# A Mamba scan beside a mixture of experts: some C products on GpSimd, and the carried state through the scan's initial value

## The chip, the cores and the metric

One core of a Trainium2 chip runs the whole program. The metric is the device time of one execution in microseconds. The runs shown took 687.11, 687.22 and 687.6 us, with a median of 687.22. One more execution was profiled; it took 687.01 us.

## The reference, cut to what matters

The input has 4 sequences of 512 steps with 256 features. The kernel computes `x + layernorm(mamba(layernorm(x)))` and then, on that, `x + layernorm(moe(layernorm(x)))`. The part that the change touches is the state-space scan of the Mamba layer (512 channels, 16 states each):

```python
def step(state, inp):
    dt_t, x_t, B_t, C_t = inp
    dA = jnp.exp(dt_t[..., None] * A)
    dBx = dt_t[..., None] * B_t[:, None, :] * x_t[..., None]
    state = state * dA + dBx
    y = jnp.einsum('bds,bs->bd', state, C_t)
    return (state, y)
```

The experts (16 with a router that keeps 4, and a shared one) compute `silu(x @ w1) * (x @ w3)`, weighted by the router and multiplied by `w2`. Every layer norm needs a mean and `(variance + eps) ** -0.5` of each row.

## The kernel before

**Blocks and slots.** The 2,048 steps are cut into 8 blocks of 256 steps (`n`); two blocks make one sequence, so the odd blocks 1, 3, 5 and 7 start from the state that the block before them left, and the even ones from zero. A block's 512 x 16 states are worked off in 32 slots (`k`). One slot is a tile of 128 partitions (32 channels times 4 states) with two columns (`j` = 0 and 1) of 256 steps, laid one behind the other.

**One slot.** `exps` (line 535, ScalarE) writes the decay `exp(dt * A)` into a PSUM tile `h`, one instruction per column, and clears the first element of column 1 (line 538), so that one scan over 512 elements restarts at the second column. `inputs_of` (line 547, GpSimd) makes `dbx`, the product of dt times x with B, for two slots at a time. `scan` (line 830, VectorE) runs in place over `h` with a start value of 0.0. `times_c` (line 838, VectorE) multiplies by C into an SBUF tile `hc`, and `sum_y` (line 852, TensorE) adds up the states. `close` and `gated_y` (lines 864 and 870) finish a group of 128 channels.

**The carried state.** In even blocks `keep` (line 842, ScalarE) copies the last element of each column into `carry`. In odd blocks `decay0`, `decay1` and `delta` (lines 817 to 824, GpSimd, ScalarE, GpSimd) multiply that state by the first decay, once for each group of 8 slots, and line 549 (GpSimd) adds the result to the first element of each `dbx` column.

**Rings.** Only three `h` tiles exist (`RINGS`, line 49), so `exps` of slot k + 3 waits for the last reader of slot k's tile, the product with C. `hc` has 11 buffers, `dbx` 3. The expert matmuls' PSUM tiles `h1` and `h3` have one buffer each.

**Around the scan.** `front(n)` prepares a block (norm, input projection, convolution, softplus). `chain(n)` follows a block's last slot: output projection, a norm, the residual, a second norm, a transposition, the router. Then `experts(n)` runs ten pairs of experts: `hidden` (line 1094, TensorE) twice, Tanh and copy (lines 1101 to 1106, ScalarE), a weight product and a gate product (lines 1109 and 1116, GpSimd) with one on VectorE between them (line 1113), and `down` (line 1129, TensorE). Experts of block n run beside the slots of block n + 1. The norms' statistics come from VectorE (line 383), and `rstd_of` makes scale and offset with four small GpSimd operations (lines 389 to 392), at 30 places.

**The order.** Every piece of work is a task with an engine, an expected duration, a rank and the tasks it depends on. The list `ORDER` (lines 58 to 215) writes out the sequence of all tasks; each engine, and the SyncE queue of DMAs, works off its part of this sequence strictly in order. `Plan.order` also models start times, from which only one thing follows: in front of the first `down`, spare matmuls (`warm`, line 355) are put where the model sees TensorE idle.

Of the kernel before, what the change touches and what calls it, by code (L numbers as in the profile page):

```python
# [14 lines left out]
P = 128  # L15
# [35 lines left out]
    tail=4, bt=2, ct=2, xg=2, rep=3, delta=3, h=3, dbx=3, hc=11, yg=2, o=1, xn2=1, xn_t2=2, lg=2,  # L51
# [7 lines left out]
    28, 304, 310, 307, 306, 305, 309, 29, 32, 314, 30, 308, 24, 311, 319, 33, 315, 15, 25, 313, 40,  # L59
    34, 320, 14, 26, 312, 31, 317, 35, 108, 324, 316, 1591, 70, 37, 12, 329, 36, 321, 27, 328, 41,  # L60
    1592, 322, 323, 325, 333, 71, 38, 330, 42, 327, 342, 72, 318, 326, 147, 39, 331, 73, 341, 334,
    43, 351, 74, 109, 332, 346, 343, 44, 303, 335, 110, 1568, 344, 1599, 336, 350, 45, 361, 381,
    347, 111, 47, 352, 345, 355, 75, 370, 340, 76, 348, 48, 16, 356, 349, 360, 337, 49, 78, 353,
    354, 358, 77, 112, 357, 79, 365, 362, 113, 369, 363, 51, 366, 80, 364, 52, 338, 384, 423, 374,
    54, 367, 371, 368, 359, 383, 375, 393, 55, 372, 376, 385, 378, 117, 339, 148, 373, 388, 57, 85,
    56, 386, 379, 377, 389, 392, 403, 58, 62, 60, 387, 86, 390, 46, 394, 53, 59, 382, 63, 50, 87,
    391, 396, 397, 380, 64, 61, 81, 412, 395, 466, 402, 398, 404, 82, 114, 149, 115, 1600, 399, 400,
    407, 65, 83, 426, 465, 405, 100, 411, 408, 1607, 116, 84, 413, 406, 410, 416, 120, 424, 409,
    101, 417, 425, 401, 414, 419, 121, 102, 468, 435, 418, 89, 415, 430, 122, 420, 427, 103, 434,
    445, 503, 139, 431, 429, 150, 421, 428, 118, 140, 454, 436, 90, 439, 91, 186, 432, 88, 433, 438,  # L70
    469, 141, 444, 470, 440, 119, 437, 124, 472, 446, 449, 441, 442, 1569, 450, 125, 142, 1608, 447,
    479, 448, 453, 443, 126, 451, 66, 458, 455, 452, 156, 471, 153, 459, 151, 152, 456, 487, 457,
    461, 67, 128, 460, 475, 68, 462, 473, 69, 478, 104, 127, 505, 422, 463, 476, 464, 467, 614, 474,
    1570, 105, 494, 480, 129, 482, 540, 477, 154, 506, 1571, 486, 507, 481, 1572, 483, 130, 490,
    106, 1573, 509, 484, 107, 155, 488, 92, 1693, 493, 1618, 491, 504, 485, 93, 1574, 489, 157, 495,
    516, 492, 496, 497, 1575, 95, 143, 187, 542, 158, 1576, 577, 498, 508, 182, 94, 499, 1577, 510,
    188, 512, 98, 1578, 500, 511, 1579, 513, 97, 144, 1580, 515, 145, 1581, 524, 99, 1582, 514,
    1583, 225, 519, 517, 1593, 189, 501, 520, 531, 1595, 1594, 1584, 523, 518, 1601, 1617, 1596,
    543, 527, 96, 544, 1585, 521, 146, 1597, 1586, 1603, 1602, 525, 579, 1587, 183, 546, 528, 530,
    1588, 1598, 526, 1589, 580, 184, 1590, 534, 1627, 522, 1604, 553, 529, 615, 131, 535, 545, 1609,  # L80
    532, 132, 1605, 1613, 533, 502, 1606, 547, 581, 561, 536, 549, 548, 178, 550, 552, 136, 1611,
    179, 551, 133, 138, 1610, 180, 1628, 537, 554, 556, 568, 190, 1612, 560, 1619, 1623, 555, 185,
    557, 191, 1637, 1614, 564, 163, 562, 195, 1620, 1615, 565, 1629, 583, 164, 558, 1633, 134, 538,
    563, 1638, 567, 1616, 165, 137, 135, 566, 590, 571, 541, 569, 159, 582, 572, 1643, 657, 1630,
    539, 559, 570, 192, 598, 584, 160, 1639, 573, 586, 161, 574, 585, 1624, 589, 587, 167, 578,
    1634, 1621, 588, 591, 605, 168, 193, 592, 1647, 593, 597, 1622, 1648, 601, 594, 123, 1625, 1631,
    1640, 1653, 599, 618, 194, 1626, 595, 1632, 604, 600, 1635, 170, 575, 1657, 608, 602, 1644, 596,
    1658, 171, 606, 166, 1636, 627, 609, 1663, 181, 603, 1649, 607, 576, 617, 173, 637, 610, 1641,
    619, 622, 1650, 611, 623, 1667, 172, 699, 621, 626, 1659, 620, 646, 1642, 631, 628, 1651, 1660,
    1668, 624, 1645, 612, 625, 636, 632, 1694, 613, 1677, 630, 638, 175, 616, 1695, 629, 640, 1654,  # L90
    641, 633, 1652, 660, 1646, 634, 1696, 645, 639, 1669, 642, 650, 1697, 647, 1678, 1661, 1673,
    1655, 1698, 643, 651, 644, 649, 1670, 1699, 1656, 1716, 659, 1662, 669, 648, 1671, 661, 1717,
    658, 1700, 663, 653, 1683, 664, 1664, 1679, 652, 741, 662, 668, 1701, 1672, 635, 665, 673, 1665,
    1724, 654, 670, 783, 667, 1680, 679, 1681, 666, 1702, 674, 678, 1703, 1674, 671, 1666, 1704,
    655, 680, 672, 676, 683, 688, 1705, 1725, 675, 1718, 687, 681, 1682, 1675, 682, 684, 1720, 1719,
    702, 685, 1732, 692, 689, 1726, 686, 784, 701, 1721, 1684, 690, 1676, 1707, 1706, 711, 693,
    1708, 691, 706, 1709, 196, 695, 694, 1733, 1710, 1685, 703, 710, 1728, 1711, 721, 705, 197, 704,
    1742, 1727, 707, 1686, 712, 709, 715, 1712, 730, 1713, 1734, 708, 1687, 716, 714, 1714, 720,
    1715, 677, 713, 234, 786, 656, 718, 787, 1729, 725, 1743, 696, 744, 722, 176, 1735, 1736, 717,
    724, 726, 1738, 1722, 1752, 217, 723, 728, 729, 753, 697, 727, 734, 1723, 1688, 731, 743, 1689,  # L100
    1748, 1744, 1737, 700, 733, 735, 1739, 1746, 732, 1745, 1762, 1754, 763, 745, 169, 737, 748,
    1753, 719, 736, 1758, 752, 746, 821, 1730, 749, 747, 757, 1740, 754, 1731, 772, 750, 756, 751,
    762, 755, 1741, 1763, 1747, 1755, 264, 758, 788, 1772, 1749, 1756, 767, 1768, 764, 1759, 218,
    759, 760, 1764, 1757, 771, 790, 768, 766, 738, 1765, 219, 765, 198, 770, 1750, 773, 1773, 776,
    698, 777, 1751, 199, 797, 742, 162, 769, 775, 739, 1782, 779, 1690, 1774, 774, 858, 200, 789,
    1760, 778, 761, 791, 793, 823, 805, 780, 1778, 792, 796, 1783, 1819, 794, 800, 740, 795, 1766,
    1691, 1775, 781, 801, 804, 782, 1692, 798, 1761, 785, 1769, 220, 799, 1818, 812, 1820, 201, 808,
    802, 1767, 806, 811, 1776, 1788, 1770, 1792, 1821, 824, 807, 1784, 1822, 1777, 815, 809, 825,
    860, 895, 827, 1786, 1785, 810, 813, 826, 1771, 1787, 1823, 1779, 814, 816, 830, 202, 834, 817,
    828, 803, 203, 1802, 1789, 1794, 829, 1793, 833, 1798, 204, 1780, 174, 831, 822, 818, 1795, 842,  # L110
    832, 206, 837, 835, 1781, 861, 207, 841, 819, 836, 1824, 838, 1841, 845, 1804, 1790, 843, 1803,
    849, 1796, 1808, 839, 1825, 848, 844, 221, 1797, 852, 1826, 850, 1806, 222, 846, 1799, 1827,
    1849, 223, 862, 1805, 1791, 1800, 1842, 847, 205, 853, 863, 864, 1828, 851, 1801, 1829, 226,
    867, 854, 227, 1843, 865, 870, 1807, 1831, 1809, 1850, 1830, 868, 1844, 1857, 1845, 933, 871,
    1832, 866, 1833, 1834, 874, 1851, 1846, 869, 897, 1835, 898, 228, 1810, 1836, 1853, 872, 1852,
    1837, 899, 879, 1838, 840, 1854, 1839, 878, 873, 1840, 1858, 209, 1867, 1847, 855, 210, 886,
    1811, 856, 875, 1863, 880, 1859, 1868, 820, 177, 882, 876, 901, 932, 229, 881, 1812, 1861, 883,
    885, 1877, 1873, 884, 889, 1848, 1855, 887, 900, 975, 908, 1813, 1856, 888, 1860, 890, 208, 904,
    1869, 1862, 1814, 230, 891, 902, 1871, 916, 1815, 905, 907, 235, 903, 1870, 1887, 1864, 906,
    911, 909, 1879, 1883, 923, 1878, 236, 910, 859, 915, 212, 877, 912, 919, 892, 1872, 857, 913,  # L120
    1865, 1881, 920, 922, 231, 936, 917, 1880, 1866, 1897, 918, 926, 921, 1874, 1893, 1889, 1882,
    215, 924, 935, 1888, 1884, 1891, 896, 925, 1875, 927, 940, 232, 1816, 893, 928, 945, 937, 1907,
    1876, 233, 1890, 938, 914, 939, 944, 1892, 211, 941, 237, 1898, 949, 894, 1903, 946, 955, 934,
    929, 950, 238, 1899, 942, 1917, 964, 943, 952, 239, 954, 1943, 947, 1944, 1900, 956, 1913, 1885,
    1017, 951, 958, 948, 959, 1909, 957, 978, 960, 963, 1901, 213, 930, 968, 1908, 961, 270, 931,
    1101, 1886, 962, 1894, 969, 1927, 1902, 987, 1945, 1910, 965, 971, 967, 966, 977, 1911, 1895,
    1946, 970, 982, 1947, 979, 1919, 1912, 1904, 1948, 983, 1896, 986, 1918, 997, 980, 1923, 981,
# [159 lines left out]
def mamba_then_moe(ctx: ExitStack, tc: tile.TileContext, a: dict, out: bass.AP):  # L287
# [241 lines left out]
    def exps(k):  # L529
# [7 lines left out]
        for j in range(1, NJ):  # L537
            S.copy(h[:, j, 0:1], zero)  # L538
# [793 lines left out]
```

## Time and profile before

| | us |
|---|---|
| median of the runs shown | 687.22 |
| profiled execution | 687.01 |
| its span, first to last instruction | 685.2 |
| first scan | 26.8 |
| last scan of blocks 0, 1, 2, 3 ends | 95.1, 163.9, 231.4, 307.2 |
| last scan of blocks 4, 5, 6, 7 ends | 380.7, 453.5, 529.0, 607.5 |
| first expert matmul of blocks 0, 1, 2, 7 | 118.4, 192.5, 269.4, 626.2 |

The span leaves out 1.8 us around it. Busy time is the time in which at least one instruction of an engine runs. Consecutive instructions of one engine often overlap by some 0.04 to 0.1 us, so the distance between two starts is a little less than the duration of one; where the second waits for the first, it is a little more (two exps of one slot last 0.478 us each and start 0.51 us apart). A float32 matmul shows as two records.

### The profile page before, as it was taken

The numbers are of one execution on the slowest core, as the hardware profiler recorded it, in microseconds if no ns is written. First come the engines' busy times: TensorE is split into PE (matmuls) and PEld (weight loads), VectorE is DVE, ScalarE is ACT, GpSimd is POOL, SyncE is SP. The second block draws the span as 40 slices with busy tenths as digits, with TensorE's granted clock in tenths as the row PEclk, the third lists the DMA queues.
The fourth block names the chain that finished last, engine by engine and source line by source line (L and its number), as shares of the span: only waits on it lengthen the run. The fifth ranks groups of instructions, "written<-read, shape, count | busy, mean of one in ns | idle before, by whom it ended". The sixth has DMA issues, their size and how long they took to land.

```text
span 685.2 us, 13305 instructions
## 1 busy us (share of the span) xinstructions
PE 669.8 (98%) x4464; PEld 540.4 (79%) x4464; DVE 573.2 (84%) x821; ACT 490.1 (72%) x1308; POOL 600.5 (88%) x607
## 2 busy tenths in 40 slices
PE   8998999999999999999999999999999999999997
PEld 7776767867887778787778678887887888878886
DVE  3699999999999999899989999999889979962112
ACT  2799889989787877877888966877767766633221
POOL 1596779999999999999999999999999999985554
PEclk9999999999999999999999999999999999999999
DMA  5395948587777786596767687696777857665561
GB/s 177 116 297 177 325 147 269 176 273 239 241 273 233 243 285 225 191 321 216 262 211 269 200 296 242 198 327 207 254 192 256 279 180 248 199 205 167 186 224 38
DMA packets 84840, 155.28 MB, mean 227 GB/s; under 512 B 9858, under 2 KB 33410, under 8 KB 84772
## 3 DMA queue, kind: packets, MB, share of 16 engines
q1 hardware_dynamic: 83940, 153.13, 67.4%
q10 hardware_dynamic: 832, 1.31, 0.5%
q8 instruction: 35, 0.57, 0.3%
q14 instruction: 33, 0.27, 0.1%
HBM read 135.40 MB, written 19.01 MB: 225 GB/s over the span
## 4 chain that ended last, share of the span: by engine, by line
PE 48%; POOL 21%; ACT 10%; DVE 9%; issue 5%; DMA 5%; SPq 1%; DVEq 0%; POOLq 0%; ACTq 0%
PE h L1094 24%; PE po L1129 11%; POOL dbx L547 10%; ACT h L535 5%; DVE h L830 4%; PE y L852 4%; POOL g L1116 4%; POOL g L1109 3%; DVE hc L838 2%; PE f L433 2%; DMA cwb<-cwd 2%; PE f L947 1%; PE f L1129 1%; PE f L355 1%; PE f L448 1%
## 5 line engine op out<-in xcount | busy, mean ns | idle before, releaser
L830 DVE TENSOR_TENSOR_SCAN h<-h,dbx 128x512 f32<-128x512 f32 x256 | 307.3, 1219 | 16.7 <-POOL dbx L549 5.4
L547 POOL TENSOR_TENSOR dbx<-rep,bt 128x1024 f32<-128x1024 f32 x127 | 300.0, 2363 | 11.6 <-DVE h L830 8.7
L1094 PE MATMUL h<-xn_t,w 128*128 128x256 f32 x1280 | 295.3, 382 | 0.5
L535 ACT ACTIVATE h<-rep,a_rep 128x256 f32<-128x256 f32 x512 | 244.9, 478 | 41.5 <-DVE hc L838 30.4
L1094 PEld LDWEIGHTS h<-xn_t,w 128*128 128x128 f32 x1280 | 240.3, 190 | 41.0 <-issue 3.3
L838 DVE TENSOR_TENSOR hc<-h,ct 128x512 f32<-128x512 f32 x256 | 170.0, 680 | 3.5 <-ACT carry L842 1.3
L1129 PE MATMUL po<-w,g 128*128 128x256 f32 x600 | 143.6, 383 | 0.6 <-POOL g L1116 0.3
L1129 PEld LDWEIGHTS po<-w,g 128*128 128x128 f32 x600 | 112.3, 190 | 21.1 <-POOL g L1116 4.2
L1116 POOL TENSOR_TENSOR g<-g,q 128x512 f32<-128x512 f32 x80 | 101.7, 1273 | 8.0 <-DVE q L1113 7.6
L1109 POOL TENSOR_TENSOR g<-g,cwb 128x512 f32<-128x512 f32 x64 | 81.2, 1273 | 13.9 <-ACT g L1106 7.7
L1113 DVE SCALAR_TENSOR_TENSOR q<-th,h 128x512 f32<-128x512 f32 x80 | 54.2, 678 | 44.8 <-PE h L1094 42.1
L1101 ACT ACTIVATE th<-h 128x512 f32<-128x512 f32 x80 | 47.6, 595 | 51.1 <-PE h L1094 46.2
L852 PE MATMUL y<-hc,sel 128*32 128x256 f32 x1024 | 65.6, 384 | 0.0
L852 PEld LDWEIGHTS y<-hc,sel 128*32 128x32 f32 x1024 | 28.6, 109 | 27.2 <-issue 10.6
L538 ACT COPY h<-zero 128x1 f32<-128x1 f32 x256 | 41.7, 163 | 8.2
L433 PE MATMUL f<-xn_t,w_in 128*128 128x256 f32 x176 | 42.2, 383 | 2.0 <-DVE gate L792 1.4
L1106 ACT COPY g<-h 128x512 f32<-128x512 f32 x64 | 37.2, 582 | 4.1 <-PE po L1129 2.9
L433 PEld LDWEIGHTS f<-xn_t,w_in 128*128 128x128 f32 x176 | 32.9, 190 | 8.3 <-DVE gate L792 1.6
L842 ACT COPY carry<-h 128x2 f32<-128x2 f32 x128 | 18.8, 160 | 18.0 <-DVE h L830 12.0
L448 PE MATMUL h<-xp,taps 64*64 64x256 f32 x288 | 29.5, 381 | 1.0 <-DVE xt L465 1.0
L448 PE MATMUL f<-xp,taps 64*64 64x256 f32 x208 | 25.3, 382 | 1.3 <-ACT xp L731 0.7
L947 PE MATMUL f<-w_out,yg 128*128 128x256 f32 x112 | 26.0, 381 | 0.0
(177 smaller groups left out, 627.3 us busy)
## 6 DMA issues: line engine op xcount, KB each, us to landing
w<-in_w SPq DMA_DIRECT2D x80, 512.0 KB, 5.0
rep<-rep SPq DMA_DIRECT2D x124, 256.0 KB, 5.0
w<-in_w SPq DMA_DIRECT2D x80, 256.0 KB, 4.3
cwb<-cwd SPq DMA_DIRECT2D x64, 256.0 KB, 5.3
xg<-xg SPq DMA_DIRECT2D x32, 256.0 KB, 5.2
bt<-bc SPq DMA_DIRECT2D x8, 512.0 KB, 5.0
ct<-bc SPq DMA_DIRECT2D x8, 512.0 KB, 6.2
xg<-xt SPq DMA_DIRECT2D x16, 256.0 KB, 4.2
```

The source lines that it names most:

```text
L433: T.matmul(t[:, j, :], w_in[:, k, ts(2 * m + j, P)], q["xn_t", n][:, k, :], start=k == 0, stop=k == CD - 1,)
L448: T.matmul(t[j][half[r ^ j], :], taps[half[r], 2 * m + j, k, :], q["pad", n, m][half[r], j, k : k + U], start=k == 0, stop=k == KC - 1,)
L535: S.activation(h[:, j, :], dt[:, m, 0, :], AF.Exp, scale=a_rep[:, c, g, m : m + 1])
L547: G.tensor_tensor(t[:, m], reps[n * CI + c][:, m, 1, :], bt[:, m], ALU.mult)
L830: V.tensor_tensor_scan(flat, flat, dbx[:, ts(p, NJ), :].rearrange("p j t -> p (j t)"), 0.0, ALU.mult, ALU.add)
L838: V.tensor_tensor(hc, expo[k], ct, ALU.mult)
L852: T.matmul(ys[n, c][m * CS : (m + 1) * CS, :], sel, hcs[k][:, j, :], start=g == 0, stop=g == SG - 1,)
L1094: T.matmul(t[:, j, :], weights[i][:, j, ts(CD * w + k, P)], x[:, k, :], start=k == 0, stop=k == CD - 1,)
L1109: G.tensor_tensor(gs[i], gs[i], cws[i], ALU.mult)
L1113: V.scalar_tensor_tensor(t, hid[i, "th"], 1.0, hid[i, 1], ALU.add, ALU.mult)
L1116: G.tensor_tensor(gs[i], gs[i], hid[i, "q"], ALU.mult)
L1129: T.matmul(acc[n][t] if n == N - 1 else acc[n][:, t, :], gs[i][:, j, ts(t, P)], weights2[i][:, j, :], start=m == 0 and j == 0 and (t == 0 ...
```

## The change

Four things change in the work itself, and the whole order is written anew.

- In blocks 0 and 1, the product with C of every fourth slot (`by_pool`, 16 of 256) is made by GpSimd. Its scan then writes into an `hc` tile in SBUF, and the product runs in place there.
- In odd blocks the scan starts from `carry` instead of 0.0, which serves column 0. For column 1 a new ScalarE step `enter` adds first decay times carried state to the first element of `dbx`, and then clears the decay's first element. `decay0`, `decay1`, `delta` and line 549 are gone.
- The first two of the four small operations of each `rstd_of` go to ScalarE (`var_of`).
- In the planner, a DMA's dependence on the DMA before it becomes a mere order (`behind`), and the tasks get new expected durations: `enter` 0.27, `exps` of odd blocks 0.97, `var_of` 0.27, the product on GpSimd 1.27 us.
- `ORDER` is a new list throughout.

```diff
-    def rstd_of(st, eps=EPS):
+    def var_of(st, eps=EPS):
+        S.activation(st[:, :, 2], st[:, :, 2], AF.Copy, scale=1.0 / D, bias=eps)
+        S.mul(st[:, :, 1], st[:, :, 1], -1.0)
+
+    def rstd_of(st):
         rstd = stat.tile([P, NU], F32, name="rstd")
         off = stat.tile([P, NU], F32, name="off")
-        G.tensor_scalar(rstd, st[:, :, 2], 1.0 / D, eps, ALU.mult, ALU.add)
-        G.tensor_scalar(off, st[:, :, 1], -1.0, None, ALU.mult)
-        G.tensor_tensor(rstd, rstd, mhalf, ALU.pow)
-        G.tensor_tensor(off, off, rstd, ALU.mult)
+        G.tensor_tensor(rstd, st[:, :, 2], mhalf, ALU.pow)
+        G.tensor_tensor(off, st[:, :, 1], rstd, ALU.mult)
...
-
+        if n % UB == 0:
+            clear(k)
+
+    def clear(k):
         for j in range(1, NJ):
-            S.copy(h[:, j, 0:1], zero)
+            S.copy(expo[k][:, j, 0:1], zero)
...
-        if n % UB:
-            G.tensor_tensor(t[:, :, 0], t[:, :, 0], deltas[n * CI + c][:, g, :], ALU.add)
+
+    def enter(k):
+
+        n, c, g, p = place(k)
+        for j in range(1, NJ):
+            m = NJ * p + j
+            x = dbxs[k // CP][:, m, 0:1]
+            S.activation(x, expo[k][:, j, 0:1], AF.Identity, bias=x, scale=carry[:, c, g, m : m + 1])
+        clear(k)
...
+    def by_pool(k):
+
+        return k < 2 * SLOTS and k % 4 == 3
 
     def scan(k):
         n, c, g, p = place(k)
         h, dbx = expo[k], dbxs[k // CP]
         flat = h.rearrange("p j t -> p (j t)")
+        to = flat
+        if by_pool(k):
+            hcs[k] = ring(work, [P, NJ, U], "hc")
+            to = hcs[k].rearrange("p j t -> p (j t)")
         V.tensor_tensor_scan(
-            flat, flat, dbx[:, ts(p, NJ), :].rearrange("p j t -> p (j t)"), 0.0, ALU.mult, ALU.add
+            to, flat, dbx[:, ts(p, NJ), :].rearrange("p j t -> p (j t)"),
+            carry[:, c, g, NJ * p : NJ * p + 1] if n % UB else 0.0, ALU.mult, ALU.add,
         )
 
     def times_c(k):
         n, c, g, p = place(k)
-        hc = hcs[k] = ring(work, [P, NJ, U], "hc")
         ct = live[n]["ct"][:, g, :].unsqueeze(1).to_broadcast([P, NJ, U])
-        V.tensor_tensor(hc, expo[k], ct, ALU.mult)
+        if by_pool(k):
+            G.tensor_tensor(hcs[k], hcs[k], ct, ALU.mult)
+        else:
+            hcs[k] = ring(work, [P, NJ, U], "hc")
+            V.tensor_tensor(hcs[k], expo[k], ct, ALU.mult)
 
     def keep(k):
         n, c, g, p = place(k)
-        S.copy(carry[:, c, g, ts(p, NJ)], expo[k][:, :, U - 1])
+        h = hcs[k] if by_pool(k) else expo[k]
+        S.copy(carry[:, c, g, ts(p, NJ)], h[:, :, U - 1])
...
+        if n % UB:
+            add(("enter", k), "ACT", 0.27, k - 1, lambda k=k: enter(k),
+                [("exps", k), ("dbx", d), ("keep", k - SLOTS)], (), [("h", k), ("dbx", d)])
+        add(("scan", k), "DVE", 1.13, k, lambda k=k: scan(k),
+            [("enter", k)] if n % UB else [("exps", k), ("dbx", d)], [("hc", ("hc", k))] if by_pool(k) else (),
             [("h", k), ("dbx", d)])
...
+        if by_pool(k):
+            add(("hc", k), "POOL", 1.27, k + 0.5, lambda k=k: times_c(k),
+                [("scan", k)] + ([] if n % UB else [("keep", k)]), (), [("hc", k), ("ct", n)])
+        else:
+            add(("hc", k), "DVE", 0.595, k + 0.5, lambda k=k: times_c(k),
+                [("scan", k)], [("hc", ("hc", k))], [("h", k), ("ct", n)])
...
-        step("rstd1", "POOL", 1.3, lambda: rstd1(4 * EPS), [own("stats1")], [("rstd", own("rstd1"))], [own("mv1")])
+        step("var1", "ACT", 0.27, lambda: var1(4 * EPS), [own("stats1")], (), [own("mv1")])
+        step("rstd1", "POOL", 0.95, rstd1, [own("var1")], [("rstd", own("rstd1"))], [own("mv1")])
...
-            add(("w13", i), "SP", 0.6, at - 10, lambda i=i: load_w(i), before("w13"),
+            add(("w13", i), "SP", 0.6, at - 10, lambda i=i: load_w(i), [list(b) for b in before("w13")],
                 [("w13", ("w13", i))], (), 512)
```

The other norms are changed as `rstd1` is, and the other loads as `w13` is.

## The prediction

> **What bounds the kernel now.** First the page: the span, and which engines are full.
>
> ```profile
> span 685.2 us, 13305 instructions
> PE 669.8 (98%) x4464; PEld 540.4 (79%) x4464; DVE 573.2 (84%) x821; ACT 490.1 (72%) x1308; POOL 600.5 (88%) x607
> ```
>
> A rule stands against the first entry. The Trainium skill (Perfetto Trace Analysis, Identifying the Most-Contended Engine) says that busy matmuls mislead, and judges by the busy share of weight loads: 79%, a fifth of PE free. The timeline decides:
>
> ```profile
> 303.27 3.62 PE L1094 MATMUL h<-xn_t,w 128*128 128x256 f32 x16
> ```
>
> Sixteen records take 3.62 us, one lasts 0.38, so they start every (3.62 - 0.38) / 15 = 0.216 us, back to back. The experts' 1,280 + 640 records at this pitch are 415 us that no other engine can shorten. By the rule, relief of POOL could take some 10 us out of the later blocks; by the pitch next to nothing. I take the pitch.
>
> Then busy times by stage: two stretches divided at the first expert matmul, then blocks 0, 1, 3 and 7 by their last scan, and what follows. Columns: stretch, length, busy time of PE, PEld, DVE, ACT, POOL.
>
> ```profile
> 0.00:118.40 118.40, 109.14 (x953) 84.88 (x953) 99.95 (x152) 92.60 (x249) 78.39 (x96) 1.00 0.66 215
> 118.40:685.00 566.60, 560.67 (x3512) 455.53 (x3512) 473.21 (x670) 397.54 (x1060) 522.15 (x512) 1.00 0.69 229
> ...
> 26.80:95.10 68.30, 62.92 (x588) 47.19 (x586) 66.31 (x88) 60.35 (x175) 53.57 (x52) 1.00 0.69 229
> 95.10:163.90 68.80, 66.93 (x513) 51.66 (x514) 67.20 (x96) 62.13 (x152) 65.05 (x71) 1.00 0.72 235
> ...
> 231.40:307.20 75.80, 75.56 (x490) 60.71 (x489) 71.26 (x101) 60.46 (x153) 73.71 (x82) 1.00 0.79 264
> ...
> 529.00:607.50 78.50, 78.18 (x457) 64.56 (x456) 69.77 (x95) 51.69 (x135) 76.53 (x82) 1.00 0.71 235
> 607.50:685.00 77.50, 72.69 (x367) 62.85 (x365) 16.41 (x38) 18.96 (x37) 42.67 (x50) 1.00 0.46 154
> ```
>
> To be seen: from 118.4 us on PE is idle 5.9 of 566.6 us, so the end is the start of the experts plus PE's own work. Before, DVE paces (66.3 of 68.3 us in block 0), and 28.8 us of PE's busy time there are spare matmuls (L355). **The prize lies in front of 118.4 us.** POOL (97% in block 3) only comes close.
>
> **The change, part by part.** These groups price it (busy, mean ns of one, idle before):
>
> ```profile
> L830 DVE TENSOR_TENSOR_SCAN h<-h,dbx 128x512 f32<-128x512 f32 x256 | 307.3, 1219 | 16.7 <-POOL dbx L549 5.4 <-ACT h L538 5.0 <-POOL dbx L547 2.5
> L838 DVE TENSOR_TENSOR hc<-h,ct 128x512 f32<-128x512 f32 x256 | 170.0, 680 | 3.5 <-ACT carry L842 1.3
> L1109 POOL TENSOR_TENSOR g<-g,cwb 128x512 f32<-128x512 f32 x64 | 81.2, 1273 | 13.9 <-ACT g L1106 7.7 <-DMA cwb<-cwd 6.0
> L465 DVE SCALAR_TENSOR_TENSOR xt<-h,chan,sig 128x256 f32<-128x256 f32 x18 | 8.3, 475 | 0.1
> L397 ACT ACTIVATE o<-f,off,rstd 128x256 f32<-128x256 f32 x14 | 7.1, 558 | 13.0 <-POOL off L392 13.0
> L1005 ACT ACTIVATE lg<-f,red 128x16 f32<-128x16 f32 x14 | 3.1, 273 | 3.1 <-DVE red L1001 3.1
> L842 ACT COPY carry<-h 128x2 f32<-128x2 f32 x128 | 18.8, 160 | 18.0 <-DVE h L830 12.0 <-DVE hc L838 5.8
> L549 POOL TENSOR_TENSOR dbx<-dbx,delta 128x4 f32<-128x4 f32 x64 | 12.8, 201 | 5.0
> ```
>
> *Products moved.* 8 of 32 per block in blocks 0 and 1 leave DVE: consecutive DVE work overlaps by 0.08 us, so 8 x 0.60 = 4.8 us less per block. POOL gets 8 x 1.23 (L1109's twin, overlapped) = 9.8 us per block; in block 0 it has 14.7 idle. Its product and `keep` now read the scan's SBUF output, so the PSUM tile is free one product (0.6 us) sooner.
>
> *Carried state on POOL.* L549 goes 64 times; with the wait that it puts behind the dbx product it costs 0.27, so 17 us; both delta products 16 x 0.37 = 6; two of four operations of each of 30 rstd chains 30 x 0.43 = 13. POOL: -36 + 19.7 = -16 us. It is not the bound, so worth nothing directly; in block 1 its queue grows from 64.0 to 68.8 us, as long as the block.
>
> *Scan with a pointer as start value.* No row shows it. Bounds: 0 [...], and what it adds in L465. DVE copies of 6 and 512 elements take 153 and 693 ns (L577, L575), so 1.07 ns per element; that leaves L838 (no pointer) 680 - 546 = 134 ns of fixed time, and L465 475 - 274 = 201: +0.06 us. I take the upper end, the nearest row: 32 x 0.06 = 1.9 us per odd block. DVE keeps 2.9 us of its gain in block 1, and loses 1.9 in blocks 3, 5, 7, where it has 4 or more idle.
>
> *`enter` on ACT, the dear part.* 128 ACTIVATEs on one column with two pointers (bias, scale), then a clear that waits for it. Without pointer 160 ns (L842); with one 273 - 15 x 0.83 = 261 (L1005); with two 558 - 255 x 0.83 = 346 (L397). So 0.346 for it, 0.03 for the wait and 0.10 until ACT is free behind the clear: 0.48 us. Before, two exps and the clear took 0.51 + 0.51 + 0.10 = 1.12 us by their starts in the timeline; after, the second exp is no longer waited for at once (0.39), and the sum is 0.51 + 0.39 + 0.48 = 1.38. The skill's rule (ScalarE: Activation LUTs, What ACT_TABLE_LOAD costs: 186 ns, and some 93 more per pointer) says 0.373, so 0.50 in place of 0.48 (0.6 us more per block); I take the row. The lower end is 0.27, for which the new order was laid out (the diff): `enter` would then leave ACT as fast as L820, 0.12 us between starts. Per odd block ACT gets 32 x 0.26 = +8.3 us, less 0.5 for four exps of L820; `var_of` adds 0.3 us in each of 30 places. Adding up ACT's queue by these pitches, between the first exp of block 1 and that of block 2, gives 61.6 us before (71.1 elapsed, 9.5 idle) and 74.5 after (8.3 - 0.5 + 1.1, and 4 that the new order moves there); in block 3 65.5, in block 7 62.1, which have room.
>
> What waits behind: `enter` stands in ACT's queue and waits for POOL's dbx and the old `keep`; behind it stand the next exps, and Tanh and copy of the experts, whose single `h1` bank PE waits for.
>
> *Queue order.* All engines are reordered, SP too, with the same 520 instructions; that the planner no longer lets a load wait for the one before it (`behind`) takes no wait out of the program, so I cost it at nothing. Counted in both built programs: until the first expert matmul PE has 92 spare matmuls instead of 102, and one `sum` less (72 instead of 80 y matmuls). In front of the first expert's gated product DVE has 43 scans and 32 products instead of 44 and 43, 7.7 us less; ACT up to evict2 of block 0 has 83.7 us instead of 81.5, with 9.9 idle before. So PE sets the start: 10 x 2 x 0.112 + 1.0 = **3.3 us earlier**. Behind the first down, mode switches of PE fall from 72 to 64, 0.09 us each: -0.7.
>
> *ACT in block 1.* Starting 4.8 us sooner (89.1 instead of 93.9), ACT needs until 89.1 + 79.0 = 168.1 us for the eighth Tanh, which came at 170.5: 2.4 us are left for idle time that was 9.5. Some of that was waiting for DVE's PSUM tiles and goes; I let PE lose 1 us.
>
> *Chains.* In front of the last experts the two rstds get 0.35 us less POOL and an ACT hop of 0.27 + 0.3: +0.5 in all; the last block's own ending is untouched.
>
> **Sum**, against the profiled execution (687.0 us: 685.2 and 1.8 around it): -3.3 + 1.0 - 0.7 + 0.5 = -2.5, so 684.5; the median of the runs shown lies 0.2 higher: **684.7 us**.
>
> **Rivals.** *Slower: ACT becomes the bound in odd blocks*, 691 us. If ACT keeps all 9.5 us of idle in block 1, the eighth Tanh comes at 177.6, 7 us late; PE's next `h1` started 1.9 to 7.7 us after the copies that free its bank there (timeline), so it loses about half, 3.5 beside the lost 3.3 (net +0.2), and in blocks 3, 5, 7 `enter`s 0.2 us behind plan cost about 1.2 us each, where the q and h1 banks are tight: 687 + 0.2 + 3.6 = 691. It decides from about 4 us of idle on. For it: order laid out for 0.27. Against: ACT at 52 to 60 of 73 to 79 us in those blocks. *No change*, 687: block 1 eats exactly the earlier start. *All of it*, 681: `enter` overlaps (0.27 holds), block 1 costs nothing, the 5.9 us of PE idle halve by POOL's relief: -3.3 - 0.7 - 2.5. That the products don't leave DVE's path is excluded by the counted orders.
>
> **Chances.** A measurement of this kernel tells 0.2% (1.4 us) from no change. My forecast 0.42 (682 to 686), slower 0.28, no change 0.20, all of it 0.10. Faster: 0.38 + 0.10 = 0.48; same 0.04 + 0.17 = 0.21; slower 0.28 + 0.03 = 0.31. Range 680.5 to 691.5, from the last rival to the slower one.
>
> **What would show it.** Right: first expert matmul near 115 us; `enter` 0.35 us; scans with pointer near 1.28; ACT over 95% in block 1; PE idle behind the start about 7 us. Wrong: `enter` far over 0.4, DVE waiting for ACT in odd blocks by more than 10 us in sum, or PE waiting for ACT copies in blocks 3, 5, 7.

## The result, and the profile after

The changed kernel takes **693.92 us** (693.81 to 694.53), the kernel before, on the same chip, 687.16 (686.57 to 687.6). The ratio is 1.0101, with a 95% interval of 1.0083 to 1.0118: about 7 us slower, where 684.7 was forecast. The page of the profiled execution:

```profile
span 692.1 us, 13374 instructions
PE 669.9 (97%) x4444; PEld 536.1 (77%) x4444; DVE 576.1 (83%) x805; ACT 529.9 (77%) x1480; POOL 591.9 (86%) x467
```

Every engine moved as the change says: ScalarE (ACT) has 40 us more to do than before (490.1), GpSimd (POOL) 9 us less. TensorE (PE) has the same busy time in a span that is 7 us longer, so it waits more. Where, the busy times by stage tell. The columns are stretch, length, and the busy time of PE, PEld, DVE, ACT and POOL; the first two rows are divided at the first expert matmul, the others are blocks 0, 1, 2, 3 and 7 by their last scans (the last row begins with the end of block 7's first scan, which here goes ahead of block 6's last).

```profile
0.00:117.10 117.10, 105.67 (x916) 81.44 (x917) 93.49 (x139) 94.53 (x266) 84.51 (x79) 1.00 0.66 221
117.10:692.10 575.00, 564.25 (x3529) 454.69 (x3528) 482.59 (x667) 435.37 (x1215) 507.38 (x389) 1.00 0.67 225
26.50:93.60 67.10, 60.69 (x574) 44.67 (x573) 62.83 (x80) 60.53 (x182) 60.21 (x47) 1.00 0.67 225
93.60:170.80 77.20, 73.35 (x521) 56.95 (x521) 67.94 (x90) 74.15 (x194) 70.93 (x54) 1.00 0.71 236
170.80:239.50 68.70, 67.99 (x431) 53.73 (x430) 67.37 (x94) 54.01 (x168) 66.59 (x52) 1.00 0.70 235
239.50:313.20 73.70, 72.41 (x475) 57.45 (x474) 69.86 (x95) 66.55 (x182) 70.94 (x54) 1.00 0.76 254
...
534.50:616.90 82.40, 82.26 (x476) 67.64 (x475) 71.79 (x95) 63.20 (x171) 72.22 (x55) 1.00 0.66 225
```

To be seen: the experts start at 117.1 us, 1.3 earlier than before, but what follows takes 575.0 us in place of 566.6, and in it TensorE is idle for 10.8 us in place of 5.9 and busy for 564.25 in place of 560.67. Block 1 is 8.4 us longer than before (68.8), with ACT busy for 74.15 of 77.2 us. The other odd blocks are less full (66.55 of 73.7 in block 3), which will matter.

The costliest of the new operations, and the scans, by shape (busy, mean ns of one, idle before):

```profile
L569 ACT ACTIVATE dbx<-h,dbx,carry 128x1 f32<-128x1 f32 x128 | 44.6, 348 | 4.1 <-POOL dbx L561 0.5 <-POOL g L1138 0.4
L848 DVE TENSOR_TENSOR_SCAN h<-h,carry,dbx 128x512 f32<-128x512 f32 x120 | 152.3, 1282 | 18.9 <-ACT h L552 16.1 <-POOL g L1138 1.2 <-POOL res L1218 0.7
L848 DVE TENSOR_TENSOR_SCAN h<-h,dbx 128x512 f32<-128x512 f32 x120 | 144.6, 1220 | 6.8 <-ACT h L552 5.3 <-POOL dbx L561 0.5 <-ACT carry L865 0.5
```

Apart from the 16 scans that write into `hc`, those of odd blocks (with `carry`) wait 16.1 us for ScalarE's clear (L552), those of even blocks 5.3. Before, all scans together waited 5.0 us for the clear. The waits (total, times, longest):

```profile
DVE h L848 <- ACT h L552: 21.3, 32, 2.5
ACT h L546 <- DVE hc L860: 14.9, 26, 2.0
POOL g L1138 <- ACT g L1135: 14.7, 4, 5.8
```

The second row was 30.4 us before: exps used to wait for VectorE, now VectorE waits for ScalarE. The third was 7.7: GpSimd waits for ScalarE's copies of the experts. The chain of work that ended last, by engine, read PE 48%, POOL 21%, ACT 10% before, and reads now:

```profile
ACT 29%; PE 28%; DVE 21%; issue 8%; POOL 8%; DMA 5%; SPq 1%; DVEq 0%; ACTq 0%; POOLq 0%
```

One slot of block 3 in the timeline (start, duration, engine):

```profile
262.18 0.36 ACT L569 ACTIVATE dbx<-h,dbx,carry 128x1 f32<-128x1 f32 x1
...
262.58 0.16 ACT L552 COPY h<-zero 128x1 f32<-128x1 f32 x1
262.68 0.98 ACT L546 ACTIVATE h<-rep,a_rep 128x256 f32<-128x256 f32 x2
...
263.69 0.35 ACT L569 ACTIVATE dbx<-h,dbx,carry 128x1 f32<-128x1 f32 x1
```

From one `enter` to the next pass 1.51 us, with ScalarE never free: two exps of 0.51, 0.40 from `enter` to the clear, 0.10 behind the clear. Over all slots the medians of the start-to-start distances are 0.51 (exp to exp), 0.51 (exp to `enter`, in the 75 of 128 slots where it follows at once), 0.38 and 0.10: **1.50 us a slot**, where the prediction has 1.38 and the kernel before 1.12. `enter` does wait for the exp ahead of it.

### The profile page after: what moved, and what is told of

It is laid out like the page before. It is cut to its first block, busy times and chain, and to the rows that moved or that the text cites. A ratio compares the mean times of both kernels' runs of the same rounds, so it can differ in the third digit from the quotient of the medians.

```text
span 692.1 us, 13374 instructions
## 1 busy us (share of the span) xinstructions
PE 669.9 (97%) x4444; PEld 536.1 (77%) x4444; DVE 576.1 (83%) x805; ACT 529.9 (77%) x1480; POOL 591.9 (86%) x467
## 4 chain that ended last, share of the span: by engine, by line
ACT 29%; PE 28%; DVE 21%; issue 8%; POOL 8%; DMA 5%; SPq 1%; DVEq 0%; ACTq 0%; POOLq 0%
PE h L1123 14%; ACT h L546 13%; DVE h L848 11%; PE po L1158 6%; DVE hc L860 6%; POOL dbx L561 3%; ACT dbx L569 2%; POOL g L1138 2%; ACT h L552 2%; PE y L875 2%; DVE q L1142 2%; ACT th L1130 2%; DMA w<-in_w 1%; POOL g L1145 1%; PE f L1158 1%
## 5 line engine op out<-in xcount | busy, mean ns | idle before, releaser
L546 ACT ACTIVATE h<-rep,a_rep 128x256 f32<-128x256 f32 x512 | 243.7, 477 | 25.9 <-DVE hc L860 14.9
L848 DVE TENSOR_TENSOR_SCAN h<-h,carry,dbx 128x512 f32<-128x512 f32 x120 | 152.3, 1282 | 18.9 <-ACT h L552 16.1
L860 DVE TENSOR_TENSOR hc<-h,ct 128x512 f32<-128x512 f32 x240 | 160.0, 682 | 4.6 <-ACT carry L865 1.2
L848 DVE TENSOR_TENSOR_SCAN h<-h,dbx 128x512 f32<-128x512 f32 x120 | 144.6, 1220 | 6.8 <-ACT h L552 5.3
L875 PE MATMUL y<-hc,sel 128*32 128x256 f32 x1024 | 64.5, 383 | 0.0
L552 ACT COPY h<-zero 128x1 f32<-128x1 f32 x256 | 41.7, 163 | 8.1
L569 ACT ACTIVATE dbx<-h,dbx,carry 128x1 f32<-128x1 f32 x128 | 44.6, 348 | 4.1 <-POOL dbx L561 0.5
```

The source lines that it names most:

```text
L546: S.activation(h[:, j, :], dt[:, m, 0, :], AF.Exp, scale=a_rep[:, c, g, m : m + 1])
L848: V.tensor_tensor_scan(to, flat, dbx[:, ts(p, NJ), :].rearrange("p j t -> p (j t)"), carry[:, c, g, NJ * p : NJ * p + 1] if n % UB else 0. ...
L860: V.tensor_tensor(hcs[k], expo[k], ct, ALU.mult)
L875: T.matmul(ys[n, c][m * CS : (m + 1) * CS, :], sel, hcs[k][:, j, :], start=g == 0, stop=g == SG - 1,)
```

## The experiments

All ratios are to the kernel before on the same chip, with 95% intervals. Edits of the changed kernel keep its order of tasks unless the text says otherwise, and edits of the kernel before keep that one's.

**Without the ACTIVATE of `enter`.** Column 1 then starts from zero in odd blocks: its carried state is left out.

```diff
-            S.activation(x, expo[k][:, j, 0:1], AF.Identity, bias=x, scale=carry[:, c, g, m : m + 1])
```

> The changed kernel without the ACTIVATE of `enter` (the carried state of column 1 is left out); the clear stays, the order too. It takes 0.348 us and the clear's wait of 0.03 off ACT, 128 times: 12 us per odd block. Theory ACT (the order was laid out for 0.27 us of `enter` and clear and gets 0.48; ACT falls behind in odd blocks, and scans, exps and expert copies with it): 684 to 687 us, DVE's waits for the clear fall from 21 us to under 8, block 1 takes 71 us or less instead of 77. Theory DVE (the pointer as start value costs 0.06 us a scan): 691 or more. Theory order (the new order is bad in itself): 691 or more.

Measured: 684.96 us, ratio 0.9967 (0.9955 to 0.9979). The 128 ACTIVATEs, 0.35 us each, cost 9 us. By stage:

```profile
0.00:116.30 116.30, 106.10 (x917) 82.08 (x918) 93.89 (x140) 92.28 (x257) 84.55 (x79) 1.00 0.68 221
116.30:682.90 566.60, 559.91 (x3529) 455.26 (x3527) 480.54 (x667) 396.43 (x1096) 506.23 (x389) 1.00 0.69 229
```

Behind the start stand 566.6 us, within 0.3 us of what the kernel before has there (566.6 to 685.0 us, 566.9 to its last instruction). The 0.8 us that remain are an earlier start. For the same 3,529 records behind the start TensorE is busy for 559.9 us in place of 564.3 and idle for 6.7 in place of 10.8. So half of the loss shows as busy time; that records which no longer follow at once overlap less (0.38 us long, 0.216 us apart when back to back) is the likely reason, not tested. The ends of the last scans tell where the 9 us lie, and VectorE's idle time in front of its scans tells what waited (us):

| last scan of block | 0 | 1 | 2 | 3 | 4 | 5 | 6 | 7 |
|---|---|---|---|---|---|---|---|---|
| changed kernel | 93.6 | 170.8 | 239.5 | 313.2 | 386.4 | 461.7 | 536.3 | 616.9 |
| without the ACTIVATE | 93.8 | 166.7 | 235.4 | 306.9 | 380.0 | 453.2 | 527.5 | 607.1 |
| lost in this block | -0.2 | 4.3 | 0.0 | 2.2 | 0.1 | 2.1 | 0.3 | 1.0 |
| idle before scans, changed kernel | 3.5 | 7.4 | 0.7 | 2.7 | 1.2 | 3.0 | 1.6 | 6.6 |
| idle before scans, without the ACTIVATE | 3.4 | 2.7 | 0.7 | 0.3 | 1.2 | 1.2 | 1.6 | 3.8 |

Only odd blocks lose, and not only block 1, where ScalarE is full. VectorE's waits in front of the scans grow in the same blocks, by 4.7, 2.4, 1.8 and 2.8 us. Of the 8.4 us by which block 1 grew against the kernel before, 4.1 stay without the ACTIVATE (72.9 against 68.8), and they cost nothing at the end; the last scans of two different orders can't be compared as simply.

**The parts beside it.** Start value 0.0 in every scan (column 0 is then scanned without its carried state):

```diff
-            carry[:, c, g, NJ * p : NJ * p + 1] if n % UB else 0.0, ALU.mult, ALU.add,
+            0.0, ALU.mult, ALU.add,
```

> The changed kernel with 0.0 as start value of every scan (the carried state of column 0 is left out), order kept. It takes 0.06 us off each of 128 scans, 7.9 us of DVE. Theory DVE: 687 to 689 us. Theory ACT: DVE waits for ACT a little longer instead, 692 to 694. Theory order: 692 to 694.

Measured: 692.72 us, ratio 1.0082 (1.0062 to 1.0102). That is 1.2 us less than with the pointer, and not clear of the noise: the four executions took 691.42 to 694.55 us, the longer the lower the granted clock (0.998 to 0.994). The profiled one started its experts at 119.0 us, with a clock of 0.96 between 80 and 120 us, and took 572.2 us behind that, 2.7 less than with the pointer. The two readings put the pointer at 1 to 3 us. The two small operations of each norm back on GpSimd:

```diff
-        S.activation(st[:, :, 2], st[:, :, 2], AF.Copy, scale=1.0 / D, bias=eps)
-        S.mul(st[:, :, 1], st[:, :, 1], -1.0)
+        G.tensor_scalar(st[:, :, 2], st[:, :, 2], 1.0 / D, eps, ALU.mult, ALU.add)
+        G.tensor_scalar(st[:, :, 1], st[:, :, 1], -1.0, None, ALU.mult)
```

> The changed kernel with the first two norm operations back on GpSimd, order kept. It takes 30 x 0.3 us off ACT and one hop off each chain in front of a norm, and gives 30 x 0.43 us back to POOL. Theory ACT: 692 to 694, since only a fifth as much leaves ACT as with `enter`, and the POOL relief is worth nothing. If the hop in the norm chains were the cause: 688 or less. Theory order: 693 to 695.

Measured: 696.18 us, ratio 1.0132 (1.0115 to 1.0148), a miss: in this order, that part of the change is worth about 2 us, although it adds 6 us to ScalarE's busy time (529.9 in place of 524.0).

**The 16 products back on VectorE**, still from and into SBUF:

```diff
-            G.tensor_tensor(hcs[k], hcs[k], ct, ALU.mult)
+            V.tensor_tensor(hcs[k], hcs[k], ct, ALU.mult)
```

> The changed kernel with the 16 C products of blocks 0 and 1 back on VectorE, where the order has them. DVE gets 16 x 0.6 us, POOL loses 16 x 1.23. If POOL's queue in blocks 0 and 1 is what delays the scans: 690 or less. Theory ACT: block 0 ends 4 us later and block 1 hardly changes, so 694 to 697.

Measured: 704.21 us, ratio 1.0244 (1.0229 to 1.026), 10 us more, where at most 3 were expected. The groups, and the 16 products alone (shortest, median, longest in ns), say why:

```profile
L860 DVE TENSOR_TENSOR hc<-h,ct 128x512 f32<-128x512 f32 x240 | 159.8, 681 | 4.1 <-ACT carry L865 0.9
L857 DVE TENSOR_TENSOR hc<-hc,ct 128x512 f32<-128x512 f32 x16 | 16.9, 1058 | 0.0
...
L857 DVE TENSOR_TENSOR hc<-hc,ct x16: 657/676/2255, 42.6 to 180.1; 128x512 f32<-128x512 f32 x16
```

The mean of 1058 ns hides two kinds. Eleven of the 16 products took 657 to 691 ns, no more than with one operand in PSUM (681). The other five took 1142 to 2255, and each of them ended some 0.55 us behind the end of a `dbx` product that was running on GpSimd. They are 6 us of VectorE that the edit itself added, by keeping both operands in SBUF. If each us counts in full, some 4 us are left for the products: an estimate, since in this order the `h` tile is free before the product.

**ScalarE's time or the scan's wait?** The ACTIVATE moved behind the clear, its output into a spare column, so that no scan waits for it (column 1's carried state is left out):

```diff
+        clear(k)
-            S.activation(x, expo[k][:, j, 0:1], AF.Identity, bias=x, scale=carry[:, c, g, m : m + 1])
-        clear(k)
+            S.activation(spare, dbxs[k // CP][:, m, 1:2], AF.Identity, bias=x, scale=carry[:, c, g, m : m + 1])
```

> The ACTIVATE of `enter` keeps its length and its place in ScalarE's queue, but stands behind the clear and writes to a spare column, so no scan waits for it; the carried state of column 1 is left out by this. Theory 1 (ScalarE's queue: the added time moves everything behind it in the queue): within 2 us of the changed kernel, 692 to 696. Theory 2 (length of the chain exps, enter, clear, scan): back to where the kernel without the ACTIVATE was, 685 to 687. In between, 688 to 691, both count.

Measured: 687.46 us, ratio 1.0009 (1.0002 to 1.0016). With ScalarE no less busy with the 128 ACTIVATEs:

```profile
L570 ACT ACTIVATE spare<-dbx,carry 128x1 f32<-128x1 f32 x128 | 49.4, 386 | 0.6 <-POOL dbx L561 0.5
...
L848 DVE TENSOR_TENSOR_SCAN h<-h,carry,dbx 128x512 f32<-128x512 f32 x120 | 151.5, 1280 | 10.5 <-ACT h L552 8.9 <-POOL g L1138 1.1
```

the scans' wait for the clear falls from 16.1 to 8.9 us, and 6.5 of the 9 us come back. ScalarE's queue gets shorter too, but only by 0.09 us a slot: exp, exp, clear, aside take 0.51 + 0.51 + 0.10 + 0.29 = 1.41 by start distances. The scan gets its tile 0.38 us earlier. In proportion to the 0.38 us that leaving the ACTIVATE out takes off the queue, 0.09 would give back 2 of 9 us, not 6.5. So most of the loss is the **length of the chain** exps, `enter`, clear, scan; the other 2.5 us go with ScalarE's time.

**Column 1 first**, so that the exp ahead of `enter` is not the one it reads:

```diff
-        for j in range(NJ):
+        for j in range(NJ)[::-1]:
```

> The changed kernel, but `exps` works column 1 before column 0, so `enter` no longer waits for the exp just ahead of it in the queue. Nothing is left out. By the chain's length: 0.1 us less in each of 128 slots, of which about half counts: 1 to 3 us faster, 691 to 693. If only the queue's busy time counts: unchanged, 693.5 to 694.5.

Measured: 694.34 us, ratio 1.0106 (1.0089 to 1.0123). It is no test of the chain: the distance from the exp to `enter` stayed at 0.51 us, since `enter` still waits for the last exp written to the tile, though that is now the other column.

**No `enter`, two scans.** In odd blocks each column is scanned by itself from its own start value, and `enter` and clear go; once in all slots, once in every second. (`split(k)` is true for odd blocks, or for their odd slots.)

```diff
+        if split(k):
+            for j in range(NJ):
+                m = NJ * p + j
+                V.tensor_tensor_scan(to[:, ts(j, U)], flat[:, ts(j, U)], dbx[:, m, :], carry[:, c, g, m : m + 1], ALU.mult, ALU.add)
+            return
```

> In odd blocks every slot is scanned in two halves of 256, each with its own carried state as start value; `enter` and its clear are gone, nothing is left out. ScalarE gets some 14 us less per odd block than in the changed kernel; VectorE gets one more fixed part of a scan, an estimate of 0.15 to 0.2 us a slot, 5 to 6.4 us per odd block. If only ScalarE's queue counts: 683 to 686. If VectorE is the bound of odd blocks (it has about 4 us to spare in blocks 3, 5, 7): 690 to 698.

> As the kernel before it, but only in every second slot of the odd blocks; the other slots keep `enter`. ScalarE gets 7 us less per odd block than in the changed kernel, VectorE 2.5 to 3.2 more. ScalarE's queue as the cause: half of the 9 us comes back or more, 686 to 689. VectorE as the bound: no better than 691.

Measured: 703.42 us, ratio 1.0237 (1.0221 to 1.0254), and 694.19 us, ratio 1.011 (1.0095 to 1.0125). In the first:

```profile
L856 DVE TENSOR_TENSOR_SCAN h<-h,carry,dbx 128x256 f32<-128x256 f32 x240 | 178.1, 751 | 5.4 <-ACT h L546 0.7 <-issue 0.2
```

A scan of 256 takes 751 ns, of 512 1282, so 220 ns of each are fixed. Now exps wait 57.6 us for VectorE's products instead of 14.9: VectorE is the bound in odd blocks. Against the kernel without the ACTIVATE it is busy for 26 us more (600.0 against 574.4), and 18 of them are paid for. Half and half, the time is that of the changed kernel.

**Addition on VectorE.** Carried state by one decay product per group as in the kernel before, but multiplied and added by VectorE right before the scan; all scans from 0.0.

```diff
+                V.tensor_tensor(deltas[i], deltas[i], carry[:, c], ALU.mult)
+            V.tensor_tensor(dbx[:, :, 0], dbx[:, :, 0], deltas[i][:, g, :], ALU.add)
```

> The changed kernel and its order, but the carried state enters as it did before the change (one decay product per group on GpSimd, one Exp on ScalarE), with the product by the carried state and the addition to the first element of `dbx` made by VectorE, right in front of the scan; all scans start from 0.0, the clear stands right behind the exps again. Nothing is left out. Theory (the `enter` in the chain exps to scan cost the 9 us): without it 685.0, less 1.2 for the start value, plus what 80 small VectorE operations of 0.15 to 0.2 us add: 684.5 to 686.5, faster than both kernels. If VectorE's own time binds in odd blocks, as when each scan was split: each added us there costs about 0.65, the net 6 us some 4: 687 to 689.

Measured: 749.62 us, ratio 1.0911 (1.0895 to 1.0928), far outside every expectation. The additions' durations (minimum, median, maximum, in ns):

```profile
L865 DVE TENSOR_TENSOR dbx<-dbx,delta x64: 140/1055/2403, 97.3 to 669.8; 128x4 f32<-128x4 f32 x64
```

Four elements take 140 ns at best, 1055 in the median, and at most 2403, about as long as one dbx product on GpSimd (2361 ns in this run). The additions are 64.5 us of VectorE. One of them in the timeline, with the GpSimd product beside it:

```profile
100.40 2.36 POOL L576 TENSOR_TENSOR dbx<-rep,bt 128x1024 f32<-128x1024 f32 x1 [0.48 <-DVE h L871]
...
101.35 1.43 DVE L865 TENSOR_TENSOR dbx<-dbx,delta 128x4 f32<-128x4 f32 x1
```

The GpSimd product ends at 102.76 us, the addition at 102.78. So it is with all of them: 16 of the 64 took 140 to 176 ns, and each of the other 48 ended 19 to 27 ns behind the end of a GpSimd instruction. The Trainium skill (SBUF — State Buffer, SBUF: two separate sides) states what this looks like: VectorE and GpSimd share a port pair as "an **exclusive lock**, not a bandwidth split", and a VectorE operation takes part in it when both its inputs lie in SBUF and GpSimd reads SBUF. This run and the five long products above agree with it. The scan, its product with C and the experts' product on VectorE each have one operand in PSUM.

**Parts alone under the old order.** The kernel before, with every fourth product of block 0 on GpSimd:

```diff
+        if by_pool(k):
+            G.tensor_tensor(hcs[k], hcs[k], ct, ALU.mult)
```

> The kernel before with one part of the change: every fourth product with C of block 0 alone on GpSimd, everything else and the order as before. VectorE loses 4.8 us of its 66 us in block 0 and GpSimd has 14.7 us of room there. If the prize lies before the first expert matmul: experts start 2 to 3.5 us earlier, 683.5 to 685.5. If the old order can't use it (its matmuls wait for something else): 686.5 to 688.

Measured: 692.78 us, ratio 1.0094 (1.0079 to 1.0109). Between 65 and 95.1 us, before the edit and with it:

```profile
65.00:95.10 30.10, 27.48 (x252) 20.20 (x251) 29.98 (x41) 26.42 (x81) 21.50 (x21) 1.00 0.74 249
```

```profile
65.00:95.10 30.10, 28.53 (x284) 21.07 (x284) 26.42 (x36) 25.88 (x76) 27.76 (x25) 1.00 0.81 265
```

VectorE has less to do (26.42 in place of 29.98) and waits, with GpSimd at 27.76 of 30.1. In this edit `keep` goes right in front of the moved product, and GpSimd's products wait for it for 5.4 us, three times, up to 3.1. The last scan of block 0 ends at 98.3 in place of 95.1, and the planner, which sees TensorE idle, adds 20 spare matmuls (244 records in place of 204, at 0.112 us each 4.5 us). Experts start at 123.4, 5 us late, and the rest of the span keeps this distance. How the late scans, the waits for `keep` and the spare matmuls share the 5 us isn't told apart. Shown is that moving these products costs 6 us in the old order, done in this way.

The kernel before with start value and `enter` instead of the decay products and the addition:

```diff
-            G.tensor_tensor(t[:, :, 0], t[:, :, 0], deltas[n * CI + c][:, g, :], ALU.add)
+        elif k // CP in dbxs:
+            enter(k)
```

> The kernel before and its order with one part of the change: start value and `enter` in place of the decay products and the addition on GpSimd (`enter` stands behind its exps or, where dbx comes later in the order, behind that). If `enter` costs by the chain that it lengthens, whatever the order: 6 to 10 us slower, 693 to 697. If the 23 us that leave GpSimd are worth more: 683 to 687.

Measured: 709.95 us, ratio 1.0336 (1.0321 to 1.0352), 23 us more, where 10 were expected at most. Here `enter` itself waits 12.5 us for GpSimd's dbx, six times, up to 4.6 us, and holds up ScalarE's queue with it.

**`enter` off the chain.** The first decay of column 1 is made apart, once per group of 8 slots; dt at the head of column 1 is set to 1000 in the replicated tile, so that its exp is zero and no clear is needed; `enter` reads the small decay and stands between the two exps. The result is whole.

```diff
+            S.activation(decays[i], decays[i], AF.Exp)
+            t = reps[n * CI + c][:, 1::NJ, 0, 0]
+            S.activation(t, t, AF.Copy, scale=0.0, bias=1000.0)
...
-            S.activation(x, expo[k][:, j, 0:1], AF.Identity, bias=x, scale=carry[:, c, g, m : m + 1])
-        clear(k)
+            S.activation(x, decays[n * CI + c][:, g, p : p + 1], AF.Identity, bias=x, scale=carry[:, c, g, m : m + 1])
```

> The changed kernel and its order, nothing left out. The decay of the first element of column 1 is made apart, once per group of 8 slots (one small GpSimd product, one Exp on ScalarE, 16 of each), and the step at the head of column 1 is set to 1000 in the replicated dt (one ScalarE copy per group), so that its exp is zero without any clear. `enter` is one ACTIVATE as before, but needs neither the exps nor a clear, and stands between the two exps. ScalarE loses 256 clears of 0.16 us, keeps 128 ACTIVATEs of 0.35 us, gets 48 small operations. Theory (the 9 us are the chain exps, enter, clear, scan; 6.5 of them its length): at most the 687.5 that the ACTIVATE off the chain cost, less the clears: 683 to 687. If the ACTIVATE's time in the queue is what costs: 690 to 693.

Measured: **685.46 us** (684.8 to 687.22), ratio 0.9981 (0.9974 to 0.9988): 8.5 us faster than the changed kernel, and by a small but measurable margin faster than the kernel before. The 128 ACTIVATEs are still there:

```profile
L591 ACT ACTIVATE dbx<-delta,dbx,carry 128x1 f32<-128x1 f32 x128 | 48.2, 376 | 5.1 <-POOL dbx L581 5.0
...
L869 DVE TENSOR_TENSOR_SCAN h<-h,carry,dbx 128x512 f32<-128x512 f32 x120 | 151.4, 1279 | 5.8 <-ACT h L564 5.6
```

The scans of odd blocks wait 5.6 us for ScalarE in place of 16.1. By start distances an odd slot takes 0.41 + 0.28 + 0.40 = 1.09 us of ScalarE from the first exp to the end of the second one's turn: instructions that don't depend on the one ahead start 0.28 to 0.41 us apart, not 0.51. The experts start at 117.8 us here, and 566.1 us follow. The chain and ScalarE's time in a slot (1.50 to 1.09 us) shrink together in this run; what tells the two apart is the run with the ACTIVATE aside.

**The clears alone**, taken out of the kernel before in the same way:

```diff
-        for j in range(1, NJ):
-            S.copy(h[:, j, 0:1], zero)
```

> The kernel before and its order, nothing left out; only the 256 clears are replaced by 32 ScalarE copies that set dt at the head of column 1 to 1000. The chain from exps to scan gets 0.1 us shorter per slot, ScalarE's busy time 36 us less. If that chain's length sets the pace in front of the first expert matmul as it does in the odd blocks of the changed kernel: 684 to 686. If VectorE alone paces block 0 and the matmuls bind behind it: 686.5 to 687.5.

Measured: 687.13 us, ratio 1.0006 (0.9999 to 1.0012). The profiled execution started its experts 1.2 us later than the kernel before, at a granted clock of 0.83 between 30 and 50 us, and took 566.4 us behind that, in place of 566.9. So behind the start 0.1 us less per slot, and 37 us less of ScalarE in all, are worth at most half a us in the kernel before: its chain has slack. In the changed kernel the clears were not taken out alone. But without the ACTIVATE and with all clears it stood at 684.96 us, so the gain of the run ahead of this one (685.46) needs no more than `enter`'s place.

**The order laid out anew.** The same kernel with `enter` off the chain, all tasks ordered twice more, independently, for the measured durations (only `ORDER` and the three durations differ).

> The kernel with `enter` off the chain, nothing left out, and the order of all tasks laid out anew for the durations that the traces show (two exps 0.91 us, with `enter` between them 1.08, scan with a pointer 1.2) in place of 1.12, 1.24 and 1.13. If the wrong durations behind the changed kernel's order still cost time: 678 to 683. If the matmuls bind and the order no longer matters: 684.5 to 686. If the new order fits the chip worse than the old one: over 686.5.

> The same kernel with a second order, laid out independently for the same durations, to see how much chance is in an order: within 1.5 us of the run before it if the durations decide, 2 us or more away if the details of an order do.

Measured: 692.29 us, ratio 1.008 (1.0068 to 1.0092), and 691.36 us, ratio 1.006 (1.0048 to 1.0073). Both are 6 to 7 us worse than the changed kernel's order under the same work; in the profiled executions 4 of them lie behind the first expert matmul (570.0 and 570.2 us in place of 566.1). Whether its wrong durations still cost time is thus not answered, and the changed kernel itself was not tried in an order laid out for its measured 1.50 us a slot; that an order which looks better by the planner's model need not be better on the chip is.

## Why the prediction was wrong, by its own steps

**TensorE full behind the start: right.** The stretch behind the first expert matmul was 566.9 us before, 566.6 without the ACTIVATE, though GpSimd had 16 us less to do in it, and 690.2 - 123.4 = 566.8 where only products of block 0 had moved. Between rule and pitch the pitch was the better guide.

**Durations: right.** `enter` 0.346 us (measured 0.348), scan with a pointer 1.28 (1.282), its price small (1 to 3 us by the run without it, where the sum has none). The estimate of `enter` takes off 0.83 ns per element; the rows give 0.85 (an exp of 256 elements with one pointer takes 478 ns, L1005 with 16 takes 273), which would make it 0.341.

**The sum for one slot: too low.** "The second exp is no longer waited for at once (0.39)" failed: where `enter` follows the exps it waits for the last of them, so such a slot is 1.50 us and not 1.38, and ScalarE gets up to 32 x 0.38 = 12 us per odd block instead of 8.3.

**The start 3.3 us earlier: half right.** TensorE's busy time before the first expert matmul fell by 3.5 us (109.14 to 105.67), as counted (the terms add up to 3.24, not 3.3). Its idle time there rose from 118.40 - 109.14 = 9.3 to 117.10 - 105.67 = 11.4, which the prediction held constant. The gain was 1.3 us; the 2 us more of idle were not traced to one cause. Without the ACTIVATE it would have been 2.1: some `enter`s of block 1 already run in front of the start.

**"I let PE lose 1 us": the step that failed.** It weighed ScalarE's added time against ScalarE's idle time, block by block, and called blocks 3, 5 and 7 safe at "52 to 60 of 73 to 79 us". Its list of what waits behind `enter` names the next exps, Tanh and the copies, but not the scan that `enter` itself holds up. They lost 2.2, 2.1 and 1.0 us, though ScalarE was busy for only 66.55 of 73.7 us in block 3 and 63.20 of 82.4 in block 7. The ACTIVATE stands between exps and scan, where VectorE, itself busy for 70 to 72 us of these blocks, waits in order: in front of the scans of blocks 1, 3, 5 and 7 it is idle for 19.7 us, and for 8.0 without the ACTIVATE. My reading is that time added there is lost at each place where the tile was just in time, however idle ScalarE is later. Shown is the sum: the run with the ACTIVATE aside puts some 6.5 us on the scans' wait and 2.5 on ScalarE's time. How the delay passes from VectorE on to TensorE was not traced place by place. By the prediction's own sum, some 2 us of the 9.2 between 684.7 and 693.9 lie in front of the first expert matmul (1.3 gained in place of 3.3), and some 7.6 behind it: 8.4 lost, where 1.0 - 0.7 + 0.5 = 0.8 was put.

**The slower rival: right in kind, low in size.** It named ScalarE in odd blocks and 691 us. It put 3.5 us on block 1 (measured 4.3) and 1.2 on each later odd block (2.2, 2.1, 1.0), and had them pass through ScalarE's queue and the experts' `q` and `h1` banks rather than through the scans. Of the signs listed, ACT over 95% in block 1 (74.15 of 77.2) stood under "right" and came true with the wrong outcome; the sign listed under "wrong", VectorE waiting for ScalarE more than 10 us in odd blocks (16.1), was the one that told, with TensorE's idle time behind the start (10.8 us, where 7 was to be right). TensorE waiting for ScalarE's copies hardly showed (2.9 us in all blocks, 1.1 before).

**GpSimd's relief "worth nothing directly": not quite.** The norm's two operations off GpSimd gained 2 us. GpSimd's busy time fell by 8.6 us in all; the 16 that were counted include waits. Whether through a shorter norm or an emptier queue wasn't tried.

## What to carry to other kernels

Idle time of an engine is slack only for work that nobody waits for. Before a small instruction is put on a half-idle engine, ask which instruction of a busier engine waits behind it, and count it as many times as it happens; if it can be fed from its own small operand, it leaves the chain and costs almost nothing. Moving work and ordering it belong together: every fourth product on GpSimd cost 6 us in the old order, while in the new one, laid out for it, taking it back cost time.

## What the hardware showed that was not expected

- A VectorE operation with both operands in SBUF can wait until a running GpSimd instruction ends: 4 elements took 140 to 2403 ns, and the 48 long ones of 64 ended 19 to 27 ns behind a GpSimd instruction; a product of 512 elements took 657 to 691 ns, or 1142 to 2255 beside a GpSimd product.
- A one-column ACTIVATE with two pointers took 348 ns with its input in PSUM, and 376 or 386 ns (two forms) with it in SBUF.
- Two exps on one tile start 0.51 us apart, though on different columns; an ACTIVATE that doesn't depend on the one ahead starts 0.28 to 0.41 us behind it.
- A scan of 512 elements with a pointer as start value takes 1282 ns, with a constant 1220; of 256, 751.
